# A fused attention and feed-forward block: the first batch's start and the last batch's end reordered

## The chip, the core and the metric

The kernel runs on one core of a Trainium2 chip. Its engines are TensorE (PE in the profile; its weight loads are listed apart as PEld), VectorE (DVE), ScalarE (ACT), GpSimd (POOL) and SyncE (SP), which here only issues DMAs. Each engine works through its own queue in order and waits on semaphores for the others. The metric is the device time of one execution in microseconds; lower is better.

## What is computed

All data are float32. `x` has 8 batches of 1024 tokens with 256 channels.

```python
xn = layernorm(x)                              # over the 256 channels
# attention part, 16 heads of 16 channels, no softmax
q, k, v = split(xn @ qkv_w + qkv_b)            # (8, 16 heads, 1024, 16) each
q, k = l2norm(q), l2norm(k)                    # q / max(sqrt(sum q*q), 1e-12)
kv = einsum('bhnd,bhne->bhde', k, v)
attn = einsum('bhnd,bhde->bhne', q, kv)        # then heads joined again
attn = attn @ proj_w + proj_b
# feed-forward part, 1024 hidden units
ffn = relu(xn @ W1 + b1) @ W2 + b2
return x + attn + ffn
```

Since there is no softmax, the attention of one batch is a product of q with a small matrix M made of k, v and `proj_w`.

## The kernel before

One batch has NT = 8 tiles of 128 tokens, two halves of HT = 4. A batch goes through these stages.

- **Normalise.** `norm_stats` takes means and variances on DVE (`bn_stats`, L226, `bn_aggr`, L228) and the root on ACT (L230); `norm_scale` inverts it on DVE; `norm_apply` writes xn, either on DVE (L254) or on ACT (L250).
- **Turn.** The products need xn with channels on the partitions. In the first batch `turn_on_pe` does this: TensorE multiplies each 128x128 block by the identity in transpose mode (L264, results tpx), and ACT copies the bank to xnT (L265). In later batches `turn` uses 32x32 transposes on DVE (L276) and DMAs (L278). For batch 1 every second of these DMAs is issued on ACT's queue, the others on SP's.
- **Project.** `project` makes q and k of one tile after another: two TensorE products into a bank pq (L316), the bias added on DVE to give qk (L320), the squares on ACT (sq, L322), and their sums per head on DVE (ss, L325). The buffer sq exists once, so the squares of a tile wait until the sums of the tile before are taken. Operations put on the list `late` come one tile later. After the fourth tile of a half come the norms of that half: a maximum on DVE (L303), a root on ACT (L304), a reciprocal on DVE (L305). `scale` multiplies q or k by the reciprocal norms (L338), k on POOL and q (through `scale_q`) on DVE.
- **Hidden.** `hidden` computes relu(xn W1 + b1) with a scheme of seven block products instead of eight (sums of the operands are prepared on POOL by `sums_of_x`, `s3_of_x`, `sums_of_w1`). For each i of 0 to 3 there are three steps: `first(i)` (products pha, phc, phd, a copy of pha on ACT, L450, and two additions on DVE, called joins here), `fifth(i)` (product phe, a join on DVE, L436, a relu on ACT, L431) and `last(i)` (second products into pha, phd and phe, each followed by a join or a relu, then four sums on POOL, L182 to L186). The steps come in the order first(0), fifth(0), first(1), last(0), fifth(1), first(2), last(1), fifth(2), first(3), last(2), fifth(3), last(3) and are numbered 0 to 11.
- **Mix.** Between the steps of `hidden` stand smaller ones. `mix_g` is xn^T k (gp, 32 TensorE records at L368), `sum_of_k` runs on POOL, `mix_kv` and `mix_m` make M. In batch 0 their places are written out in `first_steps`, with the normalisation and the turning of batch 1; in later batches in `later_steps`.
- **Second.** `second` adds up relu(...) W2 and q M in four banks poa, poc, pod and poe by the same scheme (L532), and adds the result to x. In the last batch a part of it goes back through TensorE (`back_on_pe`, tpo) and straight into x in SBUF (L591), which is stored in two halves (L633).

The order on every engine is the order in which the program is written. The PSUM pool has seven banks for everything but the mix. Before the loop over batches the first batch is prepared by hand: x arrives in four pieces, the first half is normalised on DVE and turned, the second half is normalised on ACT; all four tiles of the first half are projected, then the second half and b1 are turned, then the other four tiles are projected:

```python
    sums_of_w1()
    project(0, (0,), False)
    turn_on_pe(xnTs[0], xns[0], "x_0", (1,))
    b1_ps = bank([P, FC], "b1_ps")
    nc.tensor.transpose(b1_ps, b1_rows, ident[:FC, :FC])
...
    sums_of_x(0)
    project(0, (1,), False)
    s3_of_x(0)
    for h in range(2):
        scale(nc.gpsimd, 0, h, 1)
```

At the end of `hidden(0)` q is turned by `turn_on_pe` as well (tpq), which needs q scaled.

Of the kernel before, what the change touches and what calls it, by code (L numbers as in the profile page):

```python
# [16 lines left out]
def kernel(  # L17
# [43 lines left out]
    S = 32  # L61
    R = P // S
    NP, HP = NT // 2, HT // 2
    LN_EPS = 1e-5
    L2_EPS = 1e-12

# [167 lines left out]
    def norm_scale(b, tiles, on_act):  # L234
        i, mv, rstd = stats[b, tiles[0]]
        nc.vector.reciprocal(rstd, rstd)
        if on_act:
            nmr = small.tile([P, NT], F32, tag="nmr", name=f"nmr_{b}_{i}")[:, : len(tiles)]
            nc.vector.scalar_tensor_tensor(nmr, mv[:, :, 0], -1.0, rstd, ALU.mult, ALU.mult)
            for t in tiles:  # L240
                stats[b, t] += (nmr,)
# [13 lines left out]
                    xn, xt, mv[:, i, 0:1], rstd[:, i : i + 1], ALU.subtract, ALU.mult  # L255
                )

    def turn_on_pe(dst, src, name, halves=(0, 1)):

        for h in halves:  # L260
            for kc in range(KC):
                tp = bank([P, HT, P], f"tp{name}_{h}_{kc}")
                for i in range(HT):
                    nc.tensor.transpose(tp[:, i, :], src[:, h * HT + i, ts(kc, P)], ident)  # L264
                nc.scalar.copy(  # L265
                    dst[:, kc, ts(h, HP), :, :].rearrange("p u m w -> p u w m"),
                    tp.rearrange("p (u w) m -> p u w m", w=2),
                )
# [22 lines left out]
            )  # L291
        next(turns["x", b])

    def project(b, halves=(0, 1), with_k=True):

        xnT = xnTs[b]
        if b not in qks:
            qks[b] = one.tile([P, NT, 2 * C], F32, tag="qk", name=f"qk_{b}")
        qk = qks[b]

        def norms(h, ss):

            nc.vector.tensor_scalar_max(ss, ss, L2_EPS * L2_EPS)  # L303
            nc.scalar.activation(ss, ss, AF.Sqrt)  # L304
            nc.vector.reciprocal(ss, ss)  # L305
            if with_k:
                scale(nc.gpsimd, b, h, 1)

        for h in halves:
            ss = work.tile([P, HT, 2 * H], F32, tag="ss", name=f"ss_{b}_{h}")  # L310
            norms_of[b, h] = ss
            for i in range(HT):
                t = h * HT + i
                pq = bank([P, 512], f"pq_{b}_{t}")
                for kc in range(KC):
                    nc.tensor.matmul(  # L316
                        pq, xnT[:, kc, t // 2, :, t % 2], wqkv_sb[:, kc, 0 : 2 * C],
                        start=(kc == 0), stop=(kc == KC - 1),
                    )
                nc.vector.tensor_tensor(qk[:, t, :], pq, qkvb_sb[:, 0 : 2 * C], ALU.add)  # L320
                sq = one.tile([P, 2 * C], F32, tag="sq", name=f"sq_{b}_{t}")
                nc.scalar.activation(sq, qk[:, t, :], AF.Square)  # L322
                while late:
                    late.pop(0)()
                late.append(lambda ss=ss, sq=sq, i=i: nc.vector.tensor_reduce(  # L325
                    ss[:, i, :], sq.rearrange("p (g d) -> p g d", d=D), AX.X, ALU.add
                ))
                if i == HT - 1:
                    late.append(lambda h=h, ss=ss: norms(h, ss))
        while late and h == 1:  # L330
            late.pop(0)()

    norms_of, late = {}, []
# [158 lines left out]
    def first_steps(b):  # L492

        lo, hi = range(HT), range(HT, NT)
        return {
            0: [lambda: load_squares(b), lambda: sum_of_k(b), lambda: norm_stats(b + 1, lo)],
            2: [lambda: norm_stats(b + 1, hi), lambda: norm_scale(b + 1, lo, True)],
            3: [lambda: mix_g(b), lambda: norm_scale(b + 1, hi, False)],
            4: [lambda: norm_apply(b + 1, lo)],
            5: [lambda: norm_apply(b + 1, hi)],  # L500
            6: [lambda: mix_kv(b)],
            7: [lambda: turn_x(b + 1), lambda: turn_x(b + 1)],
            8: [lambda: turn_x(b + 1), lambda: turn_x(b + 1)],
            9: [lambda: mix_m(b)],
            10: [lambda: scale_q(b, 0), lambda: scale_q(b, 1)],
            11: [lambda: load(b + 2)],
        }

# [28 lines left out]
    def second(b):  # L537
# [55 lines left out]
            )  # L593

        a, c_, d, e = (bank([P, HP, P, 2], f"po{s}_{b}") for s in "acde")
        product(a, b11, a11, True, False)
        u1 = tmp("u1")
        nc.scalar.copy(u1, a)
        product(c_, t2, s2, True, True)
        u2 = add(tmp("u2"), c_, u1)  # L600
        product(d, t3, s3, True, False)
        u3 = add(tmp("u3"), d, u2)

        product(e, t1, s1, True, False)
        if b < B - 1:
# [12 lines left out]
        if b < B - 1:  # L618
            product(d, t4, a22, False, True)
            join(1, 0, d, u2)  # L620
            store(1)
        else:
            back_on_pe(1, y22, range(HP), "o22")
            y21 = tmp("y")
            for u in range(HP):
                product(d[:, u], t4, [r[:, u] for r in a22], False, True)
            for u in range(HP):
                nc.vector.scalar_tensor_tensor(
                    y21[:, u], d[:, u], ob[:, 2, 0:1], u2[:, u], ALU.add, ALU.add
                )  # L630
            for u in range(HP):
                back_on_pe(0, y21, (u,), f"o21_{u}")
                nc.sync.dma_start(  # L633
                    out=rows_v(out, b, 1)[:, ts(u, 2), :],
                    in_=xs[b][:, HT + 2 * u : HT + 2 * u + 2, :],
                )
        yield

    norm_stats(0, range(0, 2))
    norm_stats(0, range(2, 4))  # L640
    xnTs[0] = big.tile([P, KC, NP, P, 2], F32, tag="xnT", name="xnT_0")
    for g in (0, 2):
        norm_scale(0, range(g, g + 2), False)
        norm_apply(0, range(g, g + 2))
    turn_on_pe(xnTs[0], xns[0], "x_0", (0,))
    for g in (4, 6):
        norm_stats(0, range(g, g + 2))
    for g in (4, 6):
        norm_scale(0, range(g, g + 2), True)
        norm_apply(0, range(g, g + 2))  # L650
    sums_of_w1()
    project(0, (0,), False)
    turn_on_pe(xnTs[0], xns[0], "x_0", (1,))
    b1_ps = bank([P, FC], "b1_ps")
# [70 lines left out]
```

## Time and profile before

| | |
|---|---|
| median of 3 runs (range) | 644.08 us (642.45 to 644.57) |
| the profiled execution | 644.33 us, span 642.5 us |
| mean granted TensorE clock | 0.996 |
| instructions | 5720 |
| HBM read, written | 19.80 MB, 8.39 MB |

The span is the time from the first to the last instruction in the trace; the execution's own time is a little longer. Where the first batch stands in time (starts on TensorE, in us from the span's start):

| TensorE | start |
|---|---|
| first turn of x (tpx) | 6.06 |
| pq_0, first projected tile | 8.32 |
| turn of the second half | 17.25 |
| pq_4, first tile of the second half | 19.95 |
| first product of hidden(0) | 26.93 |
| mix_g (gp) | 37.31 |
| first(2) (pha_2) | 45.08 |
| last product into phe of hidden(0) | 63.53 |
| turn of q (tpq) | 65.39 |
| pq_0 of batch 1 | 67.89 |

A line of the timeline gives the start in us, the busy time of the group in us, the engine, the line, the operation, out<-in with shapes, the number of instructions, and in brackets the idle time before it with what ended it. A float32 product of 512 columns appears as two matmul records, and a record's busy time includes the end of its pipeline, so the records of back-to-back products overlap. In the table of stretches each engine has its busy time and, in parentheses, its number of instructions.

### The profile page before, as it was taken

The page shows a single profiled execution, that of the slowest core. Times are in us where ns is not written, and L with a number is a line of the kernel's source. Part 1 is how long each engine was busy: PE and PEld are TensorE (multiplying, and loading weights), DVE is VectorE, ACT ScalarE, POOL GpSimd, SP SyncE. Part 2 cuts the span into 40 slices and gives each one's busy share as a digit, 9 for nine tenths or more (in the row PEclk, how much of TensorE's full clock was granted, in tenths as well). Part 3 has the DMA queues.
Part 4 walks back from the last instruction along what each step waited for, and adds up shares of the span by engine and source line. Part 5 has one row for each costly group of instructions (what it writes and reads, how often), then busy time and mean ns, then how long its engine had stood idle before and what let it go on. Part 6 is the DMA issues. An engine that isn't in the chain of part 4 may idle for free.

```text
span 642.5 us, 5720 instructions
## 1 busy us (share of the span) xinstructions
PE 626.7 (98%) x1699; PEld 316.0 (49%) x1699; DVE 377.0 (59%) x658; ACT 201.4 (31%) x341; POOL 367.4 (57%) x309
## 2 busy tenths in 40 slices
PE   6998999999999999999999999999999999999997
PEld 3454546444465445554464444644446444455444
DVE  5657644677356673476645764368635677316833
ACT  4342513153032530335203442214413253003500
POOL 3473976296373972647835585537746298173901
PEclk9999999999999999999999999999999999999999
DMA  8612200471004600156002630037100450003202
GB/s 267 110 41 62 70 1 0 111 176 42 1 21 124 172 12 1 42 138 149 1 0 64 169 94 0 2 98 192 39 1 8 124 126 5 0 0 99 66 0 65
DMA packets 139502, 43.24 MB, mean 67 GB/s; under 512 B 135880, under 2 KB 136272, under 8 KB 139472
## 3 DMA queue, kind: packets, MB, share of 16 engines
q1 hardware_dynamic: 137296, 42.37, 26.1%
q10 hardware_dynamic: 2176, 0.52, 0.3%
q8 instruction: 13, 0.21, 0.1%
q14 instruction: 17, 0.14, 0.1%
HBM read 19.80 MB, written 8.39 MB: 44 GB/s over the span
## 4 chain that ended last, share of the span: by engine, by line
PE 94%; DVE 3%; DMA 1%; ACT 1%; issue 0%; SPq 0%; ACTq 0%; DVEq 0%
PE pq L316 17%; PE pod L532 11%; PE poe L532 11%; PE poa L532 11%; PE gp L368 9%; PE phe L424 8%; PE pha L424 8%; PE phd L424 8%; PE poc L532 5%; PE phc L424 4%; PE kvp L385 1%; PE mp L402 1%; DVE ss L325 1%; PE kvp L381 1%; DMA x<-in_L_attn_x_dram 1%; DVE hT L436 0%
## 5 line engine op out<-in xcount | busy, mean ns | idle before, releaser
L569 POOL TENSOR_TENSOR xq<-xq,yt_o 128x512 f32<-128x512 f32 x30 | 37.9, 1263 | 144.9 <-DVE yt_o L564 144.9
L316 PE MATMUL pq<-wqkv_sb,xnT 128*128 128x512 f32 x256 | 113.5, 602 | 1.5 <-ACT xnT L265 1.5
L431 ACT ACTIVATE hT<-hT,b_sb 128x512 f32<-128x512 f32 x96 | 68.6, 721 | 60.5 <-DVE hT L436 56.1
L182 POOL TENSOR_TENSOR hS<-hT 128x512 f32<-128x512 f32 x31 | 46.8, 1511 | 66.5 <-ACT hT L431 66.5
L316 PEld LDWEIGHTS pq<-wqkv_sb,xnT 128*128 128x128 f32 x256 | 50.8, 199 | 61.3 <-issue 58.0
L424 PE MATMUL pha<-xnT,w_sb 128*128 128x512 f32 x128 | 65.4, 592 | 0.0
L322 ACT ACTIVATE sq<-qk 128x512 f32<-128x512 f32 x64 | 40.3, 630 | 78.6 <-DVE ss L325 71.2
L320 DVE TENSOR_TENSOR qk<-pq,qkvb_sb 128x512 f32<-128x512 f32 x64 | 43.6, 681 | 32.7 <-PE pq L316 29.8
L532 PE MATMUL poa<-hT,w_sb 128*128 128x512 f32 x128 | 57.5, 592 | 0.0
L368 PE MATMUL gp<-qk,xn 128*128 128x256 f32 x256 | 56.6, 379 | 0.0
L368 PEld LDWEIGHTS gp<-qk,xn 128*128 128x128 f32 x256 | 48.7, 190 | 10.0 <-issue 3.8
L436 DVE TENSOR_TENSOR hT<-phe,u 128x512 f32<-128x512 f32 x64 | 43.8, 684 | 9.3 <-PE phe L424 7.4
L325 DVE TENSOR_REDUCE ss<-sq 128x32 f32<-128x512 f32 x64 | 43.5, 679 | 7.6 <-ACT sq L322 6.8
L564 DVE STREAM_TRANSPOSE yt_o<-y_o 128x512 f32<-128x512 f32 x30 | 32.9, 1095 | 16.6 <-ACT y_o L613 14.3
L184 POOL TENSOR_TENSOR hS<-hT,hS 128x512 f32<-128x512 f32 x31 | 39.5, 1273 | 2.4
L183 POOL TENSOR_TENSOR hS<-hS,hT 128x512 f32<-128x512 f32 x31 | 39.4, 1270 | 2.4
L450 ACT COPY u<-pha 128x512 f32<-128x512 f32 x32 | 18.4, 574 | 69.1 <-PE pha L424 66.2
L186 POOL TENSOR_TENSOR hT<-hT 128x512 f32<-128x512 f32 x31 | 39.9, 1286 | 0.0
L338 POOL TENSOR_TENSOR qk<-qk,ss 128x1024 f32<-128x1024 f32 x16 | 30.8, 1933 | 13.8 <-DVE ss L305 13.8
L230 ACT ACTIVATE rstd<-mv,eps_sb 128x8 f32<-128x8 f32 (+2 forms) x12 | 3.6, 298 | 111.5 <-DVE mv L228 110.8
L532 PEld LDWEIGHTS poa<-hT,w_sb 128*128 128x128 f32 x128 | 24.3, 190 | 27.6 <-issue 26.0
L424 PE MATMUL phe<-xS,w_sb 128*128 128x512 f32 x64 | 33.8, 611 | 3.4 <-DVE hT L436 3.4
(115 smaller groups left out, 1003.1 us busy)
## 6 DMA issues: line engine op xcount, KB each, us to landing
xq<-in_L_attn_x_dram SPq DMA_DIRECT2D x60, 128.0 KB, 3.0
out_dram<-xq SPq DMA_DIRECT2D x60, 128.0 KB, 2.4
x<-in_L_attn_x_dram SPq DMA_DIRECT2D x14, 512.0 KB, 6.1
qT<-turn_q SPq DMA_DIRECT2D x112, 64.0 KB, 2.1
xnT<-turn_x SPq DMA_DIRECT2D x104, 64.0 KB, 2.1
x<-in_L_attn_x_dram SPq DMA_DIRECT2D x4, 256.0 KB, 4.0
w_sb<-in_L_ffn_W_dram SPq DMA_DIRECT2D x2, 512.0 KB, 7.5
w_sb<-in_L_ffn_W_dram SPq DMA_DIRECT2D x8, 128.0 KB, 3.1
```

The lines of the kernel that those rows point to most:

```text
L182: eng.tensor_tensor(s1, a21, a22, ALU.add)
L184: eng.tensor_tensor(s4, a12, s2, ALU.subtract)
L186: eng.tensor_tensor(a21, a11, a21, ALU.subtract)
L316: nc.tensor.matmul(pq, xnT[:, kc, t // 2, :, t % 2], wqkv_sb[:, kc, 0 : 2 * C], start=(kc == 0), stop=(kc == KC - 1),)
L320: nc.vector.tensor_tensor(qk[:, t, :], pq, qkvb_sb[:, 0 : 2 * C], ALU.add)
L322: nc.scalar.activation(sq, qk[:, t, :], AF.Square)
L325: late.append(lambda ss=ss, sq=sq, i=i: nc.vector.tensor_reduce(ss[:, i, :], sq.rearrange("p (g d) -> p g d", d=D), AX.X, ALU.add))
L368: nc.tensor.matmul(gp[:, f, :], xn[:, t, ts(f, P)], qk[:, t, C : 2 * C], start=(t == 0), stop=(t == NT - 1),)
L424: nc.tensor.matmul(dst, lhsT, rhs, start=start, stop=stop, skip_group_check=True)
L431: nc.scalar.activation(block(i, n, m), src, AF.Relu, bias=b1_sb[:, fc : fc + 1])
L436: nc.vector.tensor_tensor(dst, p, q, ALU.add)
L532: nc.tensor.matmul(dst, l, r, start=start and n == 0, stop=stop and n == len(lhs) - 1, skip_group_check=True,)
```

## The change

- **Start.** Before x is there, TensorE turns the identity 20 times into a bank called warm.
- **Turn of the first half.** Of the two copies to xnT, the second goes to DVE instead of ACT.
- **Turn of the second half.** It comes after the third projected tile instead of the fourth, together with b1's turn and `sums_of_x`.
- **Norms of batch 0.** The maximum, root and reciprocal of both halves, and the scaling of k on POOL, leave `project` and come after step 0 of `hidden(0)`, behind the joins of `first(0)`.
- **Steps of hidden(0).** `sum_of_k` and the statistics of batch 1 move from step 0 to step 1, `mix_g` from step 3 to step 4, the scaling of q from step 10 to step 4.
- **Last batch.** The bank pod becomes two banks (pod and pof), each with 256 of the 512 columns, also for its first product and the join behind it.

Later batches keep their order: their norms stand in `project` as before.

```diff
-    def turn_on_pe(dst, src, name, halves=(0, 1)):
+    def turn_on_pe(dst, src, name, halves=(0, 1), copies=(nc.scalar.copy, nc.scalar.copy)):
...
-                nc.scalar.copy(
+                copies[kc](
...
-    def project(b, halves=(0, 1), with_k=True):
+    def project(b, between={}, with_norms=True):
...
-                if i == HT - 1:
-                    late.append(lambda h=h, ss=ss: norms(h, ss))
-        while late and h == 1:
+                if i == HT - 1 and with_norms:
+                    late.append(lambda h=h: norms(b, h))
+                between.get(t, lambda: None)()
+        while late:
             late.pop(0)()
...
+    def norms(b, h):
+
+        ss = norms_of[b, h]
+        nc.vector.tensor_scalar_max(ss, ss, L2_EPS * L2_EPS)
+        nc.scalar.activation(ss, ss, AF.Sqrt)
+        nc.vector.reciprocal(ss, ss)
+        scale(nc.gpsimd, b, h, 1)
...
-            0: [lambda: load_squares(b), lambda: sum_of_k(b), lambda: norm_stats(b + 1, lo)],
+            0: [lambda: load_squares(b), lambda: norms(b, 0), lambda: norms(b, 1)],
+            1: [lambda: sum_of_k(b), lambda: norm_stats(b + 1, lo)],
             2: [lambda: norm_stats(b + 1, hi), lambda: norm_scale(b + 1, lo, True)],
-            3: [lambda: mix_g(b), lambda: norm_scale(b + 1, hi, False)],
-            4: [lambda: norm_apply(b + 1, lo)],
+            4: [
+                lambda: mix_g(b), lambda: norm_scale(b + 1, hi, False),
+                lambda: norm_apply(b + 1, lo), lambda: scale_q(b, 0), lambda: scale_q(b, 1),
+            ],
...
-            10: [lambda: scale_q(b, 0), lambda: scale_q(b, 1)],
...
+        ds = [d] if b < B - 1 else [d[:, 0], bank([P, HP, P, 2], f"pof_{b}")[:, 1]]
+        parts = [slice(0, HP)] if b < B - 1 else range(HP)
...
-        product(d, t3, s3, True, False)
-        u3 = add(tmp("u3"), d, u2)
+        u3 = tmp("u3")
+        for du, u in zip(ds, parts):
+            product(du, t3, [r[:, u] for r in s3], True, False)
+            add(u3[:, u], du, u2[:, u])
...
-                product(d[:, u], t4, [r[:, u] for r in a22], False, True)
+                product(ds[u], t4, [r[:, u] for r in a22], False, True)
...
+    warm = bank([P, HT, P], "warm")
+    for i in range(WARM):
+        nc.tensor.transpose(warm[:, i % HT, :], ident, ident)
...
-    turn_on_pe(xnTs[0], xns[0], "x_0", (0,))
+    turn_on_pe(xnTs[0], xns[0], "x_0", (0,), (nc.scalar.copy, nc.vector.tensor_copy))
...
-    project(0, (0,), False)
-    turn_on_pe(xnTs[0], xns[0], "x_0", (1,))
-    b1_ps = bank([P, FC], "b1_ps")
-    nc.tensor.transpose(b1_ps, b1_rows, ident[:FC, :FC])
     b1_sb = const.tile([P, FC], F32, tag="b1", name="b1_sb")
-    nc.vector.tensor_copy(b1_sb, b1_ps)
-    sums_of_x(0)
-    project(0, (1,), False)
+
+    def second_half():
+        turn_on_pe(xnTs[0], xns[0], "x_0", (1,))
+        b1_ps = bank([P, FC], "b1_ps")
+        nc.tensor.transpose(b1_ps, b1_rows, ident[:FC, :FC])
+        nc.vector.tensor_copy(b1_sb, b1_ps)
+        sums_of_x(0)
+
+    project(0, {HT - 2: second_half}, False)
     s3_of_x(0)
-    for h in range(2):
-        scale(nc.gpsimd, 0, h, 1)
```

`WARM` is 20.

More of the change, by code (lines that the diff above doesn't have):

```diff
@@ L63 @@
     NP, HP = NT // 2, HT // 2
+    WARM = 20
     LN_EPS = 1e-5
@@ L299, in project @@
         qk = qks[b]
[L301 to L309, printed above, removed]
+        late = []
+        for h in range(2):
             ss = work.tile([P, HT, 2 * H], F32, tag="ss", name=f"ss_{b}_{h}")
@@ L327, in project @@
                 ))
-                if i == HT - 1:
-                    late.append(lambda h=h, ss=ss: norms(h, ss))
-        while late and h == 1:
+                if i == HT - 1 and with_norms:
+                    late.append(lambda h=h: norms(b, h))
+                between.get(t, lambda: None)()
+        while late:
             late.pop(0)()
-    norms_of, late = {}, []
+    norms_of = {}
+    def norms(b, h):
[4 more added lines that the diff above has]
+        scale(nc.gpsimd, b, h, 1)
     def scale(eng, b, h, s):
@@ L625, in second @@
             for u in range(HP):
-                product(d[:, u], t4, [r[:, u] for r in a22], False, True)
+                product(ds[u], t4, [r[:, u] for r in a22], False, True)
             for u in range(HP):
                 nc.vector.scalar_tensor_tensor(
-                    y21[:, u], d[:, u], ob[:, 2, 0:1], u2[:, u], ALU.add, ALU.add
+                    y21[:, u], ds[u], ob[:, 2, 0:1], u2[:, u], ALU.add, ALU.add
                 )
```

## The prediction

> **What bounds the kernel now.** I read the shares first, then the waits of TensorE, then the rows at each wait. Shares and chain, from the page:
>
> ```profile
> PE 626.7 (98%) x1699; PEld 316.0 (49%) x1699; DVE 377.0 (59%) x658; ACT 201.4 (31%) x341; POOL 367.4 (57%) x309
> ...
> PE 94%; DVE 3%; DMA 1%; ACT 1%; issue 0%; SPq 0%; ACTq 0%; DVEq 0%
> ```
>
> TensorE is the bound: only time in which it waits, or works slowly, can be won. Who it waited for (total us, times, longest us):
>
> ```profile
> PE tpx L264 <- DVE xn L254: 6.1, 1, 6.1
> PE phe L424 <- DVE hT L436: 3.4, 2, 2.4
> PE pq L316 <- ACT xnT L265: 1.5, 1, 1.5
> PE tpo L586 <- DVE y_o L628: 0.6, 1, 0.6
> PE phd L424 <- DVE u L436: 0.2, 1, 0.2
> ```
>
> In the timeline all but the 0.6 (at the end, 637.6) lie before 63.53; from there to 632 TensorE never waits. So the first batch decides, and what TensorE has won at its next projection (pq of batch 1, from 68.06) should reach the end. The slow work shows in the weight loads of pq and in the table of stretches (PE, PEld, DVE, ACT, POOL busy, granted clock, DMA share, GB/s):
>
> ```profile
> 10.20 0.34 PEld L316 LDWEIGHTS pq<-wqkv_sb,xnT 128*128 128x128 f32 x1 [0.52 <-issue]
> 11.05 0.34 PEld L316 LDWEIGHTS pq<-wqkv_sb,xnT 128*128 128x128 f32 x1 [0.52 <-issue]
> ...
> 12.96 0.20 PEld L316 LDWEIGHTS pq<-wqkv_sb,xnT 128*128 128x128 f32 x1 [0.23 <-issue]
> 13.39 0.20 PEld L316 LDWEIGHTS pq<-wqkv_sb,xnT 128*128 128x128 f32 x1 [0.23 <-issue]
> ```
>
> and
>
> ```profile
> 62.00:63.00 1.00, 0.00 (x0) 0.00 (x0) 1.00 (x3) 0.00 (x0) 0.00 (x0) 1.00 0.78 200
> 63.00:64.00 1.00, 0.47 (x1) 0.47 (x2) 1.00 (x2) 0.17 (x1) 0.00 (x0) 0.75 0.76 192
> 64.00:65.00 1.00, 1.00 (x2) 0.21 (x2) 1.00 (x2) 1.00 (x2) 0.00 (x0) 0.50 1.10 216
> 65.00:66.00 1.00, 1.00 (x4) 0.60 (x3) 1.00 (x2) 1.00 (x3) 0.80 (x1) 0.50 0.78 279
> 66.00:67.00 1.00, 1.00 (x7) 1.00 (x6) 0.94 (x2) 1.00 (x3) 0.92 (x2) 0.54 1.02 397
> ```
>
> Pairs of load and multiply are 0.86 us apart at first and 0.43 from 12.3 on: half clock until then (the table's own clock column says 1.00 there; the spacing decides). After the 2.35 us wait before 63.53 the granted clock falls to 0.50 until 66.9. A 512-column product is two records, so 0.86 us at full clock.
>
> **The change, part by part.** The sum runs along TensorE.
>
> *To pq_4 (before: 19.95).* The 20 added turns of the identity can start at 1.4, after the identity's last write (1.30). One turn takes 0.275 us at half clock (six in 1.65 from 6.82) and 0.121 at full (eight from 17.25 to 18.22), so they end between 3.8 and 6.9; x allows the first real turn at 6.06 and the fourth at 7.1. They cost at most some 0.6 us (first copy of xnT at 8.1 instead of 7.65, and its successor) and should bring full clock before 12.3. With full clock at about 7: fourth turn 7.3, copy of 0.62 to about 8.3, then the twelve records of pq_0 to pq_2, 12 x 0.43 = 5.15, to 13.5. The second half is now turned here: its xn was ready at 11.80; the copy that moves to DVE (0.69, by the like DVE reading of a bank at L320) stands ahead of its statistics, which start about 1.1 later, so about 12.8, still before 13.5. Eight turns, b1 and pq_3: 0.97 + 0.2 + 1.71, to 16.4. pq_4 needs the two copies on ACT; queued ahead of them are sq_0 to sq_2, each tied to a DVE reduction through the single sq buffer (0.63 + 0.68 + gaps = 1.4 a tile): sq_2 ends at about 16.3, the first copy at 16.9. So pq_4 starts at about 17.0: **2.95 won**, 0.6 of the 1.5 wait left.
>
> *To pha_2 (before: 45.08).* Sixteen records, 6.86, to 23.84; then eleven products (fifth(1) now comes before mix_g), 9.43, to 33.3; gp, 32 x 0.216 = 6.91, to 40.3. **4.8 won**: the waits 0.22 and 1.04 and their refills go. For this the joins must be in time. The sums of squares end about 26.7; before, the norms stood between them and the joins. Now two joins (1.4) come first, then both norms (maximum 0.23, root 0.31, reciprocal 0.95, hand-overs: 3.0), then the join of phe_0 at about 31.0 to 31.7; TensorE wants it at 31.55: 0.2 left. The scalings of k on POOL (1.93 each, started by the reciprocals) end at about 33.4, and gp needs the second half only four steps (1.7 us) after 33.3: hidden, 1.6 to spare.
>
> One rule speaks against this order. The row first:
>
> ```profile
> 23.30 1.23 DVE L303 TENSOR_SCALAR ss<-ss 128x128 f32<-128x128 f32 x1
> 31.23 0.23 DVE L303 TENSOR_SCALAR ss<-ss 128x128 f32<-128x128 f32 x1
> 23.17 1.27 POOL L184 TENSOR_TENSOR xS<-xnT,xS 128x512 f32<-128x512 f32 x1
> ```
>
> The same maximum takes 0.23, or 1.23 when POOL is in an addition (it ends 0.09 after POOL does). The Trainium skill, "SBUF — State Buffer", section "SBUF: two separate sides", says why: DVE and GpSimd share a port pair, and the first to start holds it for its whole instruction. The second maximum is now followed or preceded, within 0.1 us, by the 1.93 us scaling of k that the first reciprocal releases. By the 0.23 row the cost is nothing; by the rule, if POOL starts first, 1.9. DVE has it next in its own queue while POOL needs a hand-over, so I take 0.23 and keep 1.9.
>
> *To the last phe of hidden(0) (before: 63.53).* This wait is a chain through ACT's queue:
>
> ```profile
> 54.81 2.94 ACTq L278 DMA_DIRECT2D xnT<-turn_x  x4
> 57.79 0.58 ACT L450 COPY u<-pha 128x512 f32<-128x512 f32 x1 [2.88 <-DMA xnT<-turn_x]
> ```
>
> Four DMA issues of turn_x hold up the copy of pha_3, then come two joins, turn_x, three more DVE operations and the join at 62.80. The change leaves this alone. From the first turn_x (54.08) to the multiply is 9.45 us either way. Relative to the end of gp the turn starts 1.5 sooner (the activation of fifth(1) no longer stands in ACT's queue between gp and the copy of pha_2), and TensorE arrives 0.86 sooner, having done fifth(1). About 1.7 of the 2.35 stays: start at 57.9, **5.65 won**.
>
> *Clock and q.* From 63.53 to 68.06 TensorE did one product and sixteen turns, 4.53 us; at full clock 0.86 + 1.94 = 2.8: **1.7 more** if the clock holds. It fell after a stretch (60.1 to 63.5, one length of the slow spell) busy for 0.92 us, 27%; with 1.7 idle, a stretch that long is at least 50% busy, and the one before 36.2, 57% busy, kept its clock. I take it that it holds; the other end is 1.7 lost. The scaling of q (2.34 on DVE) had the turns of q wait (64.65; 0.6). Behind fifth(1) it runs from about 39.2 to 41.6 under gp; queued behind it is the join of pha_2, which can't start before 43.6: hidden. Were its two halves held up by POOL's additions (1.27 each), it would be 0.5 late on DVE, within later slack. Left where it was, TensorE would have met it.
>
> *Later.* No matmul of batches 1 to 6 moves. The nearest margin is POOL: the sum of qT that poc wants at 89.36 was there at 85.55; POOL's run begins with the activations behind the DMA issues, 5.6 to 6 sooner against TensorE's 7.3, so about 2 of 3.8 remain. SP's order is unchanged; x of batch 1 is asked for 1 us later and used at 30.
>
> *End.* The first product into pod is 20 records of 256 columns instead of 10 of 512; the closing one was already so: 4.33 against 4.29, 0.04 lost. With its own bank, the first half of y_o (0.50) runs under the second half's multiplies, where it stood on the path; but SP is issuing the other store until 638.26, so the stores (638.60 to 639.44) move only 0.35. Bounds: 0 and 0.5.
>
> **Sum.** 5.65 + 1.7 + 0.35 - 0.04 = 7.65. The same working on the kernel as it is gives 67.7 for the 68.06, so I add 0.4 for small hand-overs that it misses: 7.25 won. The profiled execution took 644.33 (span 642.5); the median 644.08 lies within its scatter. **Forecast 637.1.**
>
> **Rivals.**
> - *Turning doesn't raise the clock.* The Trainium skill, "TensorE: Matmul & The Clock Gate", "Part 4: PE-mode transpose", says that turns don't count as busy in the way multiplies do and don't bring full clock. For it: from 6.06 to 8.89 TensorE was mostly turning, and 12.3 was still the switch. Against: the slow spell from 63.5 ended at 66.9 with its last 1.5 us in turns only. By the rule full clock stays at 12.3, pq_0 starts at 9.1 and pq_4 at 18.8, 1.8 to 2.1 less: 639.0. I hold it nearly as likely as the forecast.
> - *A lock or the clock takes some back.* The maximum behind POOL (1.9), or the clock falling again in the 1.7 us wait (1.7): 638.9 to 639.
> - *The gain stops later.* TensorE arrives at pq of batch 1 at 60.7; its xnT lands 2.1 us after the last issue, about 57.8. Transfers 3 us later than now, or POOL's margin gone, would leave 2 to 4: 640 to 642.
> - *Slower: full clock doesn't come to stay.* The turns and the one-tile bursts with waits between (pq_4, phe_0) would leave no stretch busy enough, and projection and hidden(0) run at half clock. Each us of work costs another us. It decides when about 9 us of multiplies more than now run slow, past pq_7: 646 and above. Against: from pq_3 to gp only gaps of 0.6 and 0.2 are expected, and the trace kept its clock over 1.5.
>
> **Chances.** Forecast 0.42, no warming 0.30, lock or clock 0.15, stopped later 0.07, slower 0.06. The forecast alone spans 635.5 to 638 (full clock between 5.5 and 8.2; end 0 to 0.5); both rivals above it add 1.9; so 635.2 to 640.3. A measurement tells 0.3% (1.9 us) from nothing, so: faster 0.90, same 0.05, slower 0.05.
>
> **What would show it.** pq's spacing 0.43 from its first pair; pq_4 at about 17, gp starting at 33 to 34, a wait of about 1.7 on phe_3 with clock 1.00 behind it, pq of batch 1 at 60 to 61 and no TensorE wait after it. I am wrong if the second maximum takes over 1 us, if poc or pq of batch 1 waits, or if spacing stays 0.86 past 9.

## The result and the profile after

| | before | after |
|---|---|---|
| median (range) | 644.04 us (642.13 to 644.57, 6 runs) | 637.62 us (637.42 to 639.22, 6 runs) |
| the profiled execution | 644.33 us, span 642.5 us | 637.43 us, span 635.7 us |
| mean granted TensorE clock in it | 0.996 | 0.999 |

The ratio is 0.9913, with a 95% interval of 0.9895 to 0.9931 (it is not the quotient of the two medians, which is 0.9900): 0.9% faster, and the median is 0.5 us above the forecast. The six executions of the kernel before are of two kinds, two near 642.3 and four near 644.3 us, and the profiled one is of the slower kind, so the half clock behind its wait on the last phe, some 1.65 us (4.36 us from there to pq_0 of batch 1, 2.71 in the changed kernel), is part of what its profile could lose. From the page of the changed kernel, the shares of the engines and the chain that ended last:

```profile
PE 626.8 (99%) x1729; PEld 319.6 (50%) x1729; DVE 380.3 (60%) x660; ACT 201.0 (32%) x340; POOL 368.7 (58%) x309
...
PE 96%; DVE 2%; DMA 1%; ACT 0%; issue 0%; ACTq 0%; DVEq 0%
```

TensorE's busy time is the same (626.7 before) although it has 30 records more (20 turns, and 10 from the split of pod), so slow work must have gone as well as waits. TensorE's waits in the changed kernel (total us, times, longest us):

```profile
PE phe L427 <- DVE hT L439: 2.1, 1, 2.1
PE warm L652 <- POOL ident masks.py:199: 1.4, 1, 1.4
PE tpo L591 <- DVE y_o L638: 0.4, 1, 0.4
PE pq L310 <- ACT xnT L266: 0.3, 1, 0.3
PE tpx L265 <- DVE xn L255: 0.2, 1, 0.2
```

Of the 3.4 us on phe the 1.04 has gone and 2.1 is left; the 1.5 before pq_4 is no longer in the list (the 0.3 on pq stands before pq_0); the 6.1 on tpx is now mostly filled with turns. The start in TensorE's timeline (start us, busy us, engine, line, operation, out<-in, count, idle before):

```profile
1.36 4.53 PE L652 MATMUL warm<-ident 128*128 128x128 f32 x20 [1.36 <-POOL ident masks.py:199]
6.00 0.66 PE L265 MATMUL tpx<-ident,xn 128*128 128x128 f32 x2
6.84 1.09 PE L265 MATMUL tpx<-ident,xn 128*128 128x128 f32 x6 [0.19 <-DVE xn L255]
8.20 5.43 PE L310 MATMUL pq<-wqkv_sb,xnT 128*128 128x512 f32 x12 [0.27 <-ACT xnT L266]
13.46 1.04 PE L265 MATMUL tpx<-ident,xn 128*128 128x128 f32 x8
```

Twelve records of pq in 5.43 us are 0.43 apart: full clock from the first pair. The turns of x, six in 1.09, are fast already (eight took 2.41 before). Then the place where before fell to half clock, as stretches (busy us of PE, PEld, DVE, ACT, POOL with counts; granted clock; DMA share; GB/s):

```profile
57.00:58.00 1.00, 0.00 (x0) 0.00 (x0) 1.00 (x2) 0.00 (x0) 0.00 (x0) 1.00 0.66 168
58.00:59.00 1.00, 0.76 (x2) 0.44 (x3) 0.78 (x2) 0.83 (x2) 0.00 (x0) 1.00 0.39 101
59.00:60.00 1.00, 1.00 (x9) 0.80 (x8) 0.60 (x1) 1.00 (x3) 0.46 (x1) 1.00 0.60 148
60.00:61.00 1.00, 1.00 (x12) 1.00 (x10) 0.10 (x1) 1.00 (x3) 0.92 (x2) 1.00 0.81 140
```

The last phe starts at 58.24 (63.53 before), and the clock stays at 1.00 behind the wait. Set beside the forecast, with starts on TensorE:

| place | before | forecast | after |
|---|---|---|---|
| pq_4 | 19.95 | 17.0 | 16.6 |
| gp | 37.31 | 33.3 | 33.13 |
| pha_2 | 45.08 | 40.3 | 40.04 |
| last phe of hidden(0), and the wait before it | 63.53, 2.35 | 57.9, 1.7 | 58.24, 2.10 |
| pq_0 of batch 1 | 67.89 | 60.7 | 60.95 |
| from there to the end of the span | 574.6 | 574.3 | 574.7 |

Everything was won before pq_0 of batch 1 (6.94 us), nothing behind it. So in the experiments this start is the reading that matters, beside the times. Six of the kernels below are the changed kernel with one part taken back, one is the kernel before with one part added, and the other five alter what was left over.

### The profile page after: what moved, and what is told of

It reads as the page before. It is cut to its first block, busy times and chain, and to the rows that moved or that the text cites. A ratio compares the mean times of both kernels' runs of the same rounds, so it can differ in the third digit from the quotient of the medians.

```text
span 635.7 us, 5783 instructions
## 1 busy us (share of the span) xinstructions
PE 626.8 (99%) x1729; PEld 319.6 (50%) x1729; DVE 380.3 (60%) x660; ACT 201.0 (32%) x340; POOL 368.7 (58%) x309
## 4 chain that ended last, share of the span: by engine, by line
PE 96%; DVE 2%; DMA 1%; ACT 0%; issue 0%; ACTq 0%; DVEq 0%
PE pq L310 17%; PE poe L537 11%; PE poa L537 11%; PE pod L537 10%; PE gp L371 9%; PE phe L427 8%; PE pha L427 8%; PE phd L427 8%; PE poc L537 5%; PE phc L427 4%; PE kvp L388 1%; PE mp L405 1%; PE pof L537 1%; PE kvp L384 1%; DMA x<-in_L_attn_x_dram 0%; DVE hT L439 0%
## 5 line engine op out<-in xcount | busy, mean ns | idle before, releaser
L310 PE MATMUL pq<-wqkv_sb,xnT 128*128 128x512 f32 x256 | 111.9, 594 | 0.3 <-ACT xnT L266 0.3
L316 ACT ACTIVATE sq<-qk 128x512 f32<-128x512 f32 x64 | 40.3, 630 | 72.8 <-DVE ss L319 66.8
L569 DVE STREAM_TRANSPOSE yt_o<-y_o 128x512 f32<-128x512 f32 x30 | 32.9, 1096 | 16.6 <-ACT y_o L623 14.4
L184 POOL TENSOR_TENSOR hS<-hS,hT 128x512 f32<-128x512 f32 x31 | 40.3, 1299 | 2.4
L277 DVE STREAM_TRANSPOSE turn_x<-xn 128x512 f32<-128x512 f32 x28 | 17.5, 681 | 33.4 <-ACT xn L251 33.4
```

What stands on the lines that cost most here:

```text
L184: eng.tensor_tensor(s2, s1, a11, ALU.subtract)
L310: nc.tensor.matmul(pq, xnT[:, kc, t // 2, :, t % 2], wqkv_sb[:, kc, 0 : 2 * C], start=(kc == 0), stop=(kc == KC - 1),)
```

## The experiments

The medians of all twelve, against runs of the kernel before on the same chip. "pq(1)" is the start of pq_0 of batch 1 in the profiled execution, "wait" the one before the last phe of hidden(0). The rows come from groups of runs in which the kernel before had medians of 643.06 (first four rows), 643.14 (next four), 644.07 (next three) and 643.88 (last), and 644.04 beside the changed kernel. Differences of less than about 1 us between medians of different groups therefore say little; the starts in the profiles say more.

| kernel | median us (range, runs) | ratio to before (95%) | wait | pq(1) |
|---|---|---|---|---|
| before + turns | 642.03 (641.36 to 644.17, 17) | 0.9983 (0.9974 to 0.9992) | 2.3 | 65.14 |
| without the turns | 640.86 (638.68 to 641.26, 6) | 0.9946 (0.9928 to 0.9964) | 2.1 | 64.80 |
| second half after the fourth tile | 639.65 (638.75 to 642.04, 6) | 0.9944 (0.9924 to 0.9964) | 2.2 | 62.24 |
| norms and steps back | 641.40 (640.96 to 642.74, 10) | 0.9972 (0.9960 to 0.9984) | 2.4 | 64.52 |
| one bank pod | 637.88 (637.50 to 639.11, 6) | 0.9927 (0.9912 to 0.9941) | 2.1 | 61.05 |
| q scaled late | 637.68 (637.50 to 639.33, 5) | 0.9924 (0.9909 to 0.9938) | 1.6 | 62.76 |
| both copies on ACT | 638.50 (636.85 to 638.66, 6) | 0.9923 (0.9909 to 0.9937) | 2.1 | 60.37 |
| first two turns on SP | 640.34 (638.60 to 643.71, 12) | 0.9964 (0.9949 to 0.9978) | none | 62.05 |
| ACT's issues later | 634.93 (634.90 to 635.29, 4) | 0.9863 (0.9848 to 0.9879) | none | 58.42 |
| ... and both copies on ACT | 634.70 (634.59 to 636.95, 4) | 0.9867 (0.9844 to 0.9889) | none | 60.44 |
| ... and 24 turns | 634.79 (634.74 to 634.85, 4) | 0.9860 (0.9842 to 0.9878) | none | 58.27 |
| ... and 12 turns | 635.89 (635.38 to 637.13, 4) | 0.9879 (0.9856 to 0.9903) | none | 60.57 |

### Do the turns raise the clock?

The turns alone, added to the kernel before:

```diff
+    warm = bank([P, HT, P], "warm")
+    for i in range(20):
+        nc.tensor.transpose(warm[:, i % HT, :], ident, ident)
     norm_stats(0, range(0, 2))
```

> The kernel before with nothing but the 20 turns of the identity added. Theory (turns alone raise the clock): pq's records 0.43 us apart from the first, pq_4 at about 17.4 instead of 19.95, and 2.2 to 2.8 us less in all (about 641.5). Rival (turns don't count as work for the clock): spacing 0.86 until 10 to 14 us, pq_4 within 0.4 of 19.95, time within 0.4 of before.

And the changed kernel without them:

```diff
-    warm = bank([P, HT, P], "warm")
-    for i in range(WARM):
-        nc.tensor.transpose(warm[:, i % HT, :], ident, ident)
```

> The changed kernel without the 20 turns of the identity. Theory: half clock returns until 10 to 14 us, pq_4 at 18.2 to 19 instead of 16.6, everything behind it 1.6 to 2.2 us later, about 639.5. Rival (the turns give nothing): within 0.4 of the changed kernel.

With the turns alone pq_0 started at 8.43 and its records were 0.43 apart; pq_4 came at 18.10 instead of 19.95, with the wait of 1.51 before it still whole. That is 1.85 us at this place, where 2.55 were expected, and the median moved by only 1.0, where 2.2 to 2.8 were expected. (pq(1) came 2.75 sooner in the profiled execution; the other 0.90 is the clock, which did not fall there as it had in the kernel before.) Without the turns, pq's twelve records took 5.99 us and pq_4 came at 18.76, 2.2 us later than in the changed kernel; pq(1) came 3.85 later and the median is 3.2 us higher. What goes beyond 2.2 comes behind the last phe. The stretches of the kernel without turns, in the same columns as above:

```profile
60.00:61.00 1.00, 0.58 (x2) 0.35 (x3) 0.96 (x2) 0.65 (x2) 0.00 (x0) 1.00 0.29 74
61.00:62.00 1.00, 1.00 (x4) 0.40 (x3) 0.06 (x1) 1.00 (x3) 0.28 (x1) 0.53 0.60 145
62.00:63.00 1.00, 1.00 (x7) 1.00 (x6) 0.63 (x1) 1.00 (x3) 1.00 (x1) 0.50 0.72 139
```

Here the wait (2.12) is as long as in the changed kernel (2.10), and yet the clock fell. So the turns are worth some 2 us by themselves; whether the clock falls behind the wait is a second thing.

The place of the wait decides it. Every trace keeps a record of the granted clock, which the views average. In each, the changes lie whole multiples of 3.413 us apart: before, up at 12.31, down at 63.51, up at 66.92 and down at 640.36, which are 15, 1 and 168 steps. The grid lies elsewhere in each execution. Here are the steps that hold the wait without turns, with the second half after the fourth tile (the next experiment) and, cut in two, in the changed kernel:

```profile
57.64:61.05 3.41, 1.29 (x4) 0.40 (x3) 3.32 (x6) 0.70 (x2) 0.00 (x0) 1.00 0.39 99
55.98:59.39 3.41, 1.40 (x4) 0.35 (x2) 3.41 (x6) 0.00 (x0) 0.00 (x0) 1.00 0.35 90
53.66:57.08 3.42, 2.48 (x6) 0.76 (x4) 3.32 (x7) 0.00 (x0) 0.00 (x0) 1.00 0.20 52
57.08:60.49 3.41, 2.25 (x14) 1.73 (x15) 2.40 (x4) 2.32 (x4) 0.95 (x1) 1.00 0.56 134
```

Without turns the whole wait lies in one step; TensorE is busy for 1.29 us of it (38%), and the clock falls at its end, 61.05. In the second row the busy time is 1.40 us (41%) and the clock held. In the changed kernel the boundary at 57.08 cuts a wait of the same length, so both steps stay at 66% or more. In the first batch of all fourteen traces no step of products alone with 38% or less kept the clock and none with 41% or more lost it. The rise keeps to the grid too. Before, the step from 5.48 to 8.89 (busy for 2.78 us) did not bring it, and the next, full one did, at 12.31. In the changed kernel the step from 2.46 to 5.88, filled with turns of the identity and nothing else, brought it at 5.88. No step busy for 82% or less brought full clock in any trace, and every one of 93% or more did.

How many turns it takes was tried on the last kernel below (the wait on the last phe gone, both copies on ACT), with 24 and with 12 instead of 20:

```diff
-    WARM = 20
+    WARM = 24
```

> The same as the run with both copies on ScalarE, with 24 turns of the identity instead of 20. The turns ended at 5.47 in the changed kernel, and x came at 5.99. Theory (the full clock has come by about the twentieth turn, and TensorE idle between the turns and x can give it back, as in one profile where it fell after 0.62 us of idle): the idle spell goes, the four turns take 0.5 to 0.9 us, pq_0 starts within 0.2 us of the run with 20, and fewer executions are late: median the same or up to 0.5 us less. Rival (four more turns stand ahead of x): pq_0 and the end 0.2 to 0.4 us later.

> The same as the run with both copies on ScalarE and ScalarE's issues later, with 12 turns of the identity instead of 20 or 24. At the slow spacing of 0.22 us they end at about 4.0, some 2 us before x. Theory (the full clock comes after a stretch of some 4 to 5.5 us busy since 1.36, and is not reached by 12 turns followed by 2 us of idle): pq_0 starts at half clock, 0.86 us a pair, as without turns, and full clock comes at 9 to 12: 1.0 to 3.0 us more than with 24 turns, 635.8 to 637.8. Rival (any early work of TensorE is enough, and the idle time behind it doesn't matter): spacing 0.43 from pq_0 on, and 634.6 to 635.0.

TensorE's timeline with 12 turns:

```profile
1.36 2.82 PE L660 MATMUL warm<-ident 128*128 128x128 f32 x12 [1.36 <-POOL ident masks.py:199]
6.25 2.50 PE L265 MATMUL tpx<-ident,xn 128*128 128x128 f32 x8 [2.06 <-DVE xn L255]
8.60 7.32 PE L315 MATMUL pq<-wqkv_sb,xnT 128*128 128x512 f32 x12
```

and with 24:

```profile
1.36 5.38 PE L660 MATMUL warm<-ident 128*128 128x128 f32 x24 [1.36 <-POOL ident masks.py:199]
6.53 1.40 PE L265 MATMUL tpx<-ident,xn 128*128 128x128 f32 x8
8.19 5.42 PE L315 MATMUL pq<-wqkv_sb,xnT 128*128 128x512 f32 x12 [0.27 <-ACT xnT L266]
```

Twelve turns and 2 us of idle time bring nothing: eight turns of x take 2.50 (2.41 in the kernel before), and the twelve records 7.32. On the grid, the steps from 2.23 to 5.64 and from 5.64 to 9.06 are busy for 57% and 81%, and the clock comes up only at 12.47. pq(1) is 2.3 us later than with 24 turns, the median 1.1 (from another group of runs). With 24 there is no idle time between the identity and x, and full clock comes at 7.16; pq_0 starts at 8.19, as with 20 turns in the changed kernel, and the four executions lie within 0.11 us of each other.

### The second half after the fourth tile again

```diff
-    project(0, {HT - 2: second_half}, False)
+    project(0, {HT - 1: second_half}, False)
```

> The changed kernel with the second half turned after the fourth projected tile, as before. Theory (the copies to xnT stand in ACT's queue behind one more tile of squares and sums, 1.4 us): pq_4 at about 18.0 instead of 16.6, 1.4 us slower (about 639.0). Rival (what holds pq_4 is the late xn, not the squares): within 0.4 of the changed kernel.

The wait before pq_4 came back (1.6 us), pq_4 started at 17.84 and gp at 34.37: 1.24 later in both places, kept as far as pq(1), 1.29. The profiled times differ by 1.3 us (638.75 and 637.43), the medians by 2.0; three of its six executions had a granted clock of 0.996 or less, against two of six of the changed kernel.

### Norms and steps back

The norms return to `project`, and `sum_of_k`, the statistics, `mix_g` and the scaling of q to their old steps:

```diff
-            0: [lambda: load_squares(b), lambda: norms(b, 0), lambda: norms(b, 1)],
-            1: [lambda: sum_of_k(b), lambda: norm_stats(b + 1, lo)],
+            0: [lambda: load_squares(b), lambda: sum_of_k(b), lambda: norm_stats(b + 1, lo)],
...
+            3: [lambda: mix_g(b), lambda: norm_scale(b + 1, hi, False)],
+            4: [lambda: norm_apply(b + 1, lo)],
...
+            10: [lambda: scale_q(b, 0), lambda: scale_q(b, 1)],
```

> The changed kernel with the norms back in the projection of batch 0 and sum_of_k, mix_g and the scaling of q back in their old steps. Theory: the waits of 0.2 and 1.0 us on the joins of last(0) return, the wait on the last phe is 2.4 again, half clock follows it in most runs; 2.2 us slower with the clock kept, up to 3.9 where it falls (640 to 641.5). Rival (the order of the steps only moves waits about): within 0.5 of the changed kernel, 637.6.

The two waits that the order had removed are back, 1.04 on phe at 32.95 and 0.26 on phd at 30.78, the last wait is 2.36, and the clock fell to 0.50 behind it. pq(1) is 3.57 us later and the median 3.8. Of the 3.57, 1.90 lie before the last phe (60.14): the two waits with what it takes to start again, and a last wait longer by 0.26. The other 1.67 lie from there to pq(1), 4.38 us instead of 2.71. The fallen clock accounts for them: the kernel without turns, where q was scaled early and the clock fell too, also took 4.38. Which of the pieces taken back here brings back which wait is not separated.

### The scaling of q, and what POOL does to it

The changed kernel's VectorE under gp, from its timeline:

```profile
38.95 4.19 DVE L341 TENSOR_TENSOR qk<-qk,ss 128x1024 f32<-128x1024 f32 x2
```

and POOL at the same time:

```profile
38.58 1.27 POOL L183 TENSOR_TENSOR hS<-hT 128x512 f32<-128x512 f32 x1 [0.64 <-ACT hT L434]
39.92 2.13 POOL L184 TENSOR_TENSOR hS<-hS,hT 128x512 f32<-128x512 f32 x1
42.13 2.14 POOL L185 TENSOR_TENSOR hS<-hT,hS 128x512 f32<-128x512 f32 x1
```

In the kernel before the scalings stood at

```profile
63.40 2.34 DVE L338 TENSOR_TENSOR qk<-qk,ss 128x1024 f32<-128x1024 f32 x2
```

The two took 2.34 there; here 4.19. POOL's additions take 1.27 when alone; here the two that lie beside the scalings take 2.13 and 2.14. They fit the Trainium skill's "SBUF — State Buffer", "SBUF: two separate sides", by which whoever comes first holds the shared port for a whole instruction; the engines then alternate: POOL until 39.85, q's first half to about 41, POOL to 42.05, q's second half to 43.14, POOL to 44.27. So POOL came to be 1.7 us late (twice 0.86), and that put its last addition (44.23) beside VectorE's `norm_apply` of the second half, which took 1.92 instead of 1.37:

```profile
44.70 1.92 DVE L255 TENSOR_SCALAR xn<-x,mv,rstd 128x256 f32<-128x256 f32 x4
```

The run that puts the scaling back to step 10 takes the two apart:

```diff
-                lambda: norm_apply(b + 1, lo), lambda: scale_q(b, 0), lambda: scale_q(b, 1),
+                lambda: norm_apply(b + 1, lo),
...
+            10: [lambda: scale_q(b, 0), lambda: scale_q(b, 1)],
```

> The changed kernel with the scaling of q back in step 10. Theory: the DVE's two scalings took 4.19 us under POOL's additions in step 4 and made the last phe wait 0.4 longer; in step 10 they take about 2.3 and the turn of q waits for them, 0.5 to 1.5 us, so 0.1 to 1.1 us slower on balance. Rival: the move costs as much as it brings, within 0.1.

There the scaling took 2.34 (at 59.16), POOL's additions 1.26 to 1.28, `norm_apply` 1.37, and the wait on the last phe was 1.56 instead of 2.10. But tpq, which needs the scaled q, took 2.40 instead of 1.91, and pq(1) came 3.46 after the last phe instead of 2.71. The two effects nearly cancel: from gp to pq(1) it took 28.03 us, and 27.82 in the changed kernel, and the medians are 637.68 and 637.62. The profiled execution of this run is 1.8 us late for another reason: the clock was at 0.50 from 8.6 to 12.0.

### The copy on VectorE and the bank pof

```diff
-    turn_on_pe(xnTs[0], xns[0], "x_0", (0,), (nc.scalar.copy, nc.vector.tensor_copy))
+    turn_on_pe(xnTs[0], xns[0], "x_0", (0,))
```

> The changed kernel with both copies of the first half on ACT. Theory: the copy on DVE gains TensorE nothing (pq_0's second product is not due before 9.06, and ACT would have the copy done at 8.75) and holds up the statistics of the second half by 1.1 us; without it xn is there 1.0 sooner, pq_4 starts at 16.2 instead of 16.6 and the kernel is 0.2 to 0.6 us faster. Rival (the copy on DVE is what lets pq_0 run through): pq_0 waits, 0.2 to 0.6 slower.

With both copies on ACT, pq_0 started 2.2 us after the first turn of x, as in the changed kernel, and pq's last twenty records took 8.86 us instead of 9.16: VectorE's statistics no longer wait behind a copy of 0.69, and the wait inside those records goes. The lowest time of the changed order's runs so far (636.85) is here, but the median is 0.9 higher, because three of the six executions had a granted clock of 0.996 or 0.997; the intervals of the ratios overlap. A gain of 0.3 is in the profile; the times alone don't show it.

```diff
-        ds = [d] if b < B - 1 else [d[:, 0], bank([P, HP, P, 2], f"pof_{b}")[:, 1]]
-        parts = [slice(0, HP)] if b < B - 1 else range(HP)
+        ds, parts = [d], [slice(0, HP)]
```

> The changed kernel with pod as one bank again in the last batch. Theory: the last multiply to the end of the span is 0.3 to 0.4 us longer, since the first half of y_o waits for the second half's multiplies; about 638.0. Rival (SP's issue of the other store sets the end anyway): within 0.1 of the changed kernel.

One bank costs 0.26 us by the medians, within the scatter, and nothing by the span behind pq(1): 574.7 in both. The 0.3 to 0.4 us expected of it are not there. The reason is on SP. Its last issues in the kernel before

```profile
635.62 2.64 SPq L578 DMA_DIRECT2D out_dram<-xq  x4
...
638.60 0.84 SPq L633 DMA_DIRECT2D out_dram<-x  x2
```

and in the changed kernel:

```profile
628.73 2.64 SPq L583 DMA_DIRECT2D out_dram<-xq  x4
...
631.47 1.08 SPq L643 DMA_DIRECT2D out_dram<-x  x2
```

Counted from the first group of four tpo turns (632.08 and 625.19), the first store of x starts at 6.52 and now at 6.28, but the second is through at 7.36 in both. VectorE's last addition ends 0.4 sooner (6.89 and 6.49), but SP doesn't pass it on: the first store of x can now only be issued 0.10 after the four others are through, and the two issues take 1.08 instead of 0.84.

### What is left: the wait on the last phe

The forecast put this wait down to ScalarE's queue: four DMA issues of `turn_x` stand ahead of the copy of pha_3. The first attempt gives all issues of the first two turns to SP:

```diff
-                queues[r % 2].dma_start(
+                (nc.sync if j < first_on_sp else queues[r % 2]).dma_start(
```

> The changed kernel with the first two turns of batch 1's x issued on SP alone and the last two shared with ACT, so that ACT's queue is free for the copy of pha_3. Theory (the wait on the last phe is made by the DMA issues on ACT): no wait on the last phe, clock 1.00 in every run, pq of batch 1 at 58.8 or, if it waits for the last DMA to land, 59.5; 1.4 to 2.1 us faster, about 636, and no more runs near 639. Rival (the wait comes from the DVE's backlog): the wait stays above 1.5.

The waits of this kernel:

```profile
PE pq L310 <- DMA xnT<-turn_x: 3.5, 1, 3.5
PE warm L652 <- POOL ident masks.py:199: 1.4, 1, 1.4
```

and SP's issues in it:

```profile
49.32 11.04 SPq L279 DMA_DIRECT2D xnT<-turn_x  x12
```

The wait on phe is gone and tpq starts at 56.67 instead of 59.20, so the cause is right. But SP needs 0.92 us for each issue, twelve of them end at 60.36, and pq(1) waits until 62.05 for what the last one brings. A wait was exchanged for a longer one, and the 1.4 to 2.1 us expected did not come. Nor did the steady runs: the profiled execution, the fastest of the twelve, kept its clock at 1.00, but ten of the others had a granted clock of 0.996 or less and took 1.6 to 5.1 us longer.

The second attempt leaves the shares as they are and only holds ScalarE's issues of the first two turns back until its copy of pha_3 is out:

```diff
-                queues[r % 2].dma_start(
-                    out=dst[ts(j, S), :, :, ts(r, S), :], in_=sq[ts(r, S), j, :, :, :, :]
-                )
+                issue = lambda j=j, r=r: queues[r % 2].dma_start(
+                    out=dst[ts(j, S), :, :, ts(r, S), :], in_=sq[ts(r, S), j, :, :, :, :]
+                )
+                if held_back is not None and j < 2 and r % 2:
+                    held_back.append(issue)
+                else:
+                    issue()
...
-            8: [lambda: turn_x(b + 1), lambda: turn_x(b + 1)],
+            8: [
+                lambda: [issue() for issue in held_back],
+                lambda: turn_x(b + 1), lambda: turn_x(b + 1),
+            ],
```

> The changed kernel with one thing moved: of batch 1's first two turns, ScalarE's four DMA issues (2.94 us at 49.46) come behind its copy of pha_3 instead of ahead of it; SyncE's half stays where it is. Nothing is left out. Theory (the copy behind the issues makes the 2.10 us wait on the last phe, and SyncE's twelve issues, not the transfers themselves, made the run with SyncE alone late): the copy is at about 49.3, the wait on the last phe goes to under 0.5, the third and fourth turn are ready at about 51.7 instead of 55.8, SyncE's eight issues end at about 57 instead of 59.07, and pq_0 of batch 1 starts at 58.8 to 59.3 instead of 60.95: 1.6 to 2.2 us less than the changed kernel, about 635.7, ratio 0.988 to 0.990. Rival (the transfers' landing sets pq_0 of batch 1 wherever the copy is): tpq comes sooner but pq_0 of batch 1 waits for xnT and starts at 60.4 or later, less than 0.6 us won.

ScalarE's timeline in this kernel:

```profile
49.32 0.57 ACT L458 COPY u<-pha 128x512 f32<-128x512 f32 x1
50.05 4.89 ACTq L279 DMA_DIRECT2D xnT<-turn_x  x7
54.99 0.69 ACT L439 ACTIVATE hT<-pha,b_sb 128x512 f32<-128x512 f32 x1 [5.11 <-DVE hT L444]
```

and SP's issues:

```profile
49.31 7.28 SPq L279 DMA_DIRECT2D xnT<-turn_x  x8
```

The copy comes at 49.32 (52.50 in the changed kernel), so the joins and with them the third and fourth turn come sooner, and SP's eight issues run without the gap: they end at 56.59 instead of 59.07. Behind the start of pq_4 TensorE has no wait up to the end of `hidden(0)`, nor at tpq or pq(1), which starts at 58.42, 2.53 sooner. The median is 634.93, 2.7 us below the changed kernel's (in the profiled executions 2.5), and more than the 1.6 to 2.2 expected. The transfers left room for the whole 2.10, and 0.16 came from an earlier x (gp at 32.97 instead of 33.13). The other 0.26 is what a stop costs besides the wait. In the changed kernel the last phe started 3.12 behind the product before it instead of 0.86, which is 2.26 more, though the list of waits counts 2.10; and tpq followed it after 0.96, here after 0.86.

With both copies on ACT as well:

> The same, and both copies of the first half's turned tiles on ScalarE as before the change. By the run of that edit alone, VectorE's copy costs 0.3 us in the start: another 0.2 to 0.4 us less than the run with ScalarE's issues later alone, some 635.4. Rival (VectorE's copy is hidden, and the 0.3 us of that run's profile were the earlier x): no difference.

634.70, 0.2 us less, with one execution of four at 636.95. The profile is of that one:

```profile
1.36 4.28 PE L660 MATMUL warm<-ident 128*128 128x128 f32 x20 [1.36 <-POOL ident masks.py:199]
6.53 0.65 PE L265 MATMUL tpx<-ident,xn 128*128 128x128 f32 x2 [0.89 <-DVE xn L255]
...
8.73 7.06 PE L315 MATMUL pq<-wqkv_sb,xnT 128*128 128x512 f32 x12 [0.27 <-ACT xnT L266]
```

TensorE was idle for 0.89 us between the identity and x, the turns of x still ran at the fast spacing, and then the clock was at 0.50 from 8.65 to 12.07. With 24 turns that idle time is filled, and none of its four executions was late. The kernel with ScalarE's issues later, both copies on ACT and 24 turns is the one to keep: **634.79 us, ratio 0.9860 (0.9842 to 0.9878)**, 2.8 us below the changed kernel's median. With 20 turns the median is the same within 0.1, but not every execution.

## Why the prediction was right, and where its terms were off

The forecast was 637.1 with a range of 635.2 to 640.3; it came to 637.62, by the mechanism that was called the likeliest. The sum was 7.25 us; the profiled executions differ by 6.90.

- **The turns raise the clock: right.** The rival that they don't, held at 0.30, is out: the kernel before with the turns alone projects at full clock from its first pair. The Trainium skill, "TensorE: Matmul & The Clock Gate", "Part 4: PE-mode transpose", says that the full clock doesn't engage for turns; in this kernel it does, after a step of the grid with nothing but turns in it, and the measurement decides. The cold turn was mis-sized, but without effect: 0.275 was read off turns of x, whose data came in pieces, and the turns of the identity are some 0.22 apart.
- **pq_4: right, 0.4 sooner than expected.** Its first copy was expected at 16.9 behind sq_2 on ScalarE; the wait left over was 0.3 instead of 0.6. Turning the second half a tile sooner is worth 1.2 to 1.3 us, shown by taking it back.
- **VectorE's copy** was counted as harmless, because the second half would be normalised by 12.8 and is needed at 13.5. It was there at 12.75; but the copy also delays the chain of sums behind it, which the step left out: 0.3 us in pq's last twenty records.
- **The second maximum: right.** It was taken at 0.23 and took 0.16, and the join of phe_0 was over at 31.26. The rule of port sharing did not bite there. It bit at q, where the forecast allowed for it and mis-sized what follows: "within later slack" was wrong. q's second half was over at 43.14, in time for the join of pha_2, but POOL's additions had become late in turn and slowed `norm_apply`, by 0.55 us, and VectorE has no slack there: it is the chain that ends in the last phe (the copy of pha_3 came 19.37 behind the start of gp, and 18.83 with the scaling elsewhere).
- **The last phe.** So 2.10 was left and not 1.7, and it started at 58.24 and not 57.9. With the scaling of q elsewhere the wait is 1.56. The 0.4 us set aside for small hand-overs covered it in size; that was luck, since it was meant for something else. Its basis was off too: 68.06 is the end of the turns of q, and pq(1) itself started at 67.89 before.
- **The clock behind the wait: the right measure, and luck in this execution.** It held, and pq(1) came 2.71 after the last phe (2.8 expected). The forecast looked at the share of busy time in a stretch of 3.4 us, and the traces bear that out, but the stretch has a fixed place on the grid, which the forecast didn't know. The 1.7 us it expected would have left 50% wherever they lay. The 2.10 that came leave 38% when they lie in one step, as in the kernel without turns, where the clock fell; here a boundary cut them. Two of the changed kernel's six executions had a granted clock of 0.996 and took 1.1 and 1.6 us longer than the median. A fall fits that, so this rival is likely real in part of the executions; where the clock fell in them was not traced.
- **q's move** was counted as won, since TensorE would otherwise have met the scaling. It would have (pq(1) 0.75 later behind the last phe), but the move costs 0.54 in the wait before; its worth is some 0.2 us.
- **The end: wrong by its 0.31.** The step named SP's issues as what limits it and then let both stores move 0.35. The first moved 0.24, the second not at all, and the end with it.
- **Later margins: right.** POOL's delays never reached TensorE: no wait from pq(1) to the closing tpo.

What stays open: where between 38% and 41% the limit for products lies, how turns count towards it, and which of the moved steps removed which of the two early waits.

## What to carry to other kernels

When a start waits for data, a stand-in job for TensorE is worth its place only if it lasts until the data are there: here 24 small turns gave steady runs, 20 mostly worked, 12 brought nothing. An estimate from the grid says why: to be sure of one full step of 3.41 us the work must last up to 6.8 us, and 20 turns lasted 3.9 to 4.5. A wait near the limit is best removed altogether, since its place on the grid changes with every execution. A DMA issue on ScalarE's queue cost 0.7 us of that queue, so what TensorE waits for must be queued ahead of it: moving four issues behind one copy brought pq(1) 2.5 us forward. When work is moved under a long product to hide it, look at the engine that shares its port as well, and at what that engine does next.

## What the runs showed of the hardware

- The clock changes only on a grid of 3.413 us. The five half-clock spells ahead of the end have its length: 63.51 to 66.92 (before), 61.05 to 64.46 (without turns), 60.15 to 63.56 (norms and steps back), 8.57 to 11.98 (q scaled late) and 8.65 to 12.07 (ACT's issues later and both copies on ACT). The Trainium skill, "TensorE: Matmul & The Clock Gate", "Part 1: The HAM clock gate (the "warmup" mystery)", gives a window of 3413 ns that runs freely; this agrees. The first rise came between 4.53 and 6.09 us in the ten traces with 20 turns.
- A spell can begin after TensorE has been idle for only 0.62 or 0.89 us (the two early ones). The step before each holds ten turns (and, with q scaled late, the first 0.17 us of pq); in ACT's issues later, with 0.56 us of idle time but thirteen turns in the step (4.53 to 7.94), the clock held.
- The slow start reads 1.00 in the clock column of the stretches, because the trace's record begins only with the first change, up to full clock (12.31 before, 5.88 after). The spacing of the records and the weight loads (0.34 and 0.20 us) show it. The later spells read 0.50.
- An issue of a 64 KB DMA took SP 0.91 us (eight in 7.28) and ScalarE 0.70 (seven in 4.89).
